# Cross-attention over 32 batches: value rows loaded in padded runs of 80 per head

## The chip, the cores and the metric

The kernel runs on one core of a Trainium2 chip. The time is the device time of one execution in microseconds (us), given as the median of several runs. A profiled execution, taken by the hardware profiler, shows what each engine did: PE multiplies matrices (PEld loads its weights), DVE, ACT and POOL work on vectors, SP issues the DMA transfers. The transfers of the core share 16 DMA engines.

## The reference

The input x is (32, 512, 640), the context (32, 77, 1024), in float32. With 20 heads of 32 columns:

```python
q = _heads(hidden_states @ to_q_w)
h_txt = _sdpa(q, _heads(ehs_txt @ to_k_w), _heads(ehs_txt @ to_v_w))
...
out = _merge(h_txt) + SCALE_OBJ * _merge(h_obj) + SCALE_OTH * _merge(h_oth) + SCALE_IP * _merge(h_ip)
out = out @ to_out_w + to_out_b
out = (out + residual) / RESCALE
```

where `_sdpa` is softmax(q k^T / sqrt(32)) v. The context has 77 rows per batch, all of which are the text part, so the object, other and image parts are empty and add zero. What remains is one attention over 77 keys per batch, a projection with bias, and the residual x.

## The kernel before, in words

Every float32 operand of a product is split into a high and a low part (`split`: ACT copies the high part, DVE or POOL subtracts it), and a product is three passes: high by high, high by low, low by high (`PAIRS`).

First stage, about the first 280 us: keys and values of all 32 x 77 = 2464 context rows, in groups of 512 rows. Weights and context are loaded (`split_weights` L103, `context` L132), the context is transposed on DVE, PE computes keys (L164) and values (L190), and both go back to memory as `k_dram` and `v_dram`. `v_dram` holds, for each row, 20 heads x 32 columns x (high, low); one head of one row is 256 bytes in one piece. This stage is ordered by a scheduler in the framework. It begins with a tile of zeros, set by DVE (L211), with which PE does twelve products that nobody reads (`warm`, L214).

Second stage: the instructions are in an order written out by hand (`manual_schedule`, L639). A slot is one batch b and one chunk j of four heads; n = 5 b + j counts 160 slots. Each engine works through its own list in this order, and SP issues all DMA transfers in this order too; an instruction that waits holds all behind it on its engine. A slot n contains, among others:

- `refill` (L507): loads of keys (`kb`) or values (`vb`) of the batch. The five chunks are in two groups (`GROUPS`: chunks 0 and 1, chunks 2 to 4), each with one buffer. At j = 1 the values of group 0 are loaded, at j = 3 those of group 1, at j = 0 and j = 2 keys.
- `cast_p` (L395) and `rest_p` (L402): the probabilities of slot n - 3, read back into `raw`, are split into `pp` by ACT (L399, L405), DVE (L406) and POOL (L409).
- four times `scores` (L329): PE computes 128 queries x 308 scores into one of three buffers `sc`, DVE takes the negated maximum per head (`nm`, L343). Behind each, `exps` (L348): ACT computes the exponentials into `pn` (L353), and their sums. The buffer `sc` comes free after that.
- `sums` and `normalize` (L361, L366): POOL divides the probabilities of slot n - 1 by their sums (L368), behind POOL's part of `rest_p`.
- `queries` (L311) of slot n + 1 on PE, `split_q` to ACT and DVE.
- `finish` (L475): DVE adds the projected rows to the residual (L481), SP stores finished rows (`out_dram`, L485). `load_residual` (L439) loads x rows into one of three buffers `xr`, POOL adds the bias (L446).
- `load_p` (L388): the probabilities of slot n - 2 are loaded from memory into `raw` (L391, L392).
- `transpose_p` (L372): DVE transposes the probabilities of slot n - 1 in blocks (`z`, L375), and four stores (L382) write them to a buffer `pd` in memory, from where `load_p` gets them with keys as rows. Each head has 80 rows there (KPAD), 77 for the keys and three of zeros: `pn` is cleared once and only 77 of its 80 columns are written.
- `values` (L417): PE multiplies `pp` with `vb` (eight passes, L423).
- `piece` (L467): PE's share of the output projection of an earlier batch (L453).
- `transpose_x` (L259) at j = 0 and 1: DVE transposes parts of x of the next batch in place, in the buffer `xs` (L261); `split_x` (L263) at j = 1 to 3 splits it. `load_x` (L251) at j = 4 loads x of the batch after the next into `xs` with four transfers (L256), behind the stores and loads of that slot.

The tile `vb` has 128 rows and, per chunk, three blocks: the 4 x 80 padded rows of the four heads fill blocks 0 and 1 and half of block 2; the other half of block 2 repeats those rows, for the low part of the probabilities. It is cleared once. `load_values` loads it by `SEGMENTS`, seven pieces of rows that belong to one head and one block:

Of the kernel before, what the change touches and what calls it, by code (L numbers as in the profile page):

```python
# [8 lines left out]
F32 = mybir.dt.float32  # L9
FPR = mybir.dt.float32r  # L10
# [13 lines left out]
P = 128  # L24
Q = 32
HEADS = 20
HD = 32
NKEY = 77
HPC = 4
KCOLS = HPC * NKEY  # L30
KPAD = 80
# [5 lines left out]
for _t in range(3):  # L37
    for _i in range(HPC):
        _lo = max(_t * P, _i * KPAD)
        _hi = min((_t + 1) * P, _i * KPAD + NKEY)  # L40
        if _lo < _hi:
            SEGMENTS.append((_t, _lo - _t * P, _i, _lo - _i * KPAD, _hi - _lo))
            if _t == 2:
                SEGMENTS.append((_t, _lo - _t * P + 64, _i, _lo - _i * KPAD, _hi - _lo))
# [6 lines left out]
def kernel(  # L51
# [24 lines left out]
    nc = tc.nc  # L76
    B, S, C = x.shape
    CA = ehs.shape[2]
    NT = B * NKEY
# [11 lines left out]
    dram = ctx.enter_context(tc.tile_pool(name="scratch", bufs=1, space=DRAM))  # L91

    k_dram = dram.tile([P, NC_, 2, NT], FPR, name="k_dram")
    v_dram = dram.tile([NT, HEADS, HD, 2], FPR, name="v_dram")
    wo_dram = dram.tile([P, NC_, 2, C], FPR, name="wo_dram")

    bias = const.tile([P, C], F32, name="bias")
# [111 lines left out]

    zero = kvt.tile([P, G], FPR, name="zero", tag="craw")  # L210
    nc.vector.memset(zero.bitcast(F32), 0.0)  # L211
    warm = psk.tile([P, G], F32, tag="ps", name="warm")
    for _ in range(12):
        nc.tensor.matmul(warm, zero[:, :P], zero, start=True, stop=True)  # L214
# [500 lines left out]
```

## Time and profile before

| | |
|---|---|
| time, median of 3 runs | 2177.66 us (2176.08 to 2178.84) |
| profiled execution | 2178.59 us |
| its span, first to last instruction | 2176.8 us |
| PE busy | 2043.0 us (94%) |
| ACT busy | 1377.9 us (63%) |
| DVE busy | 1230.4 us (57%) |
| POOL busy | 1051.7 us (48%) |
| 16 DMA engines, the queue of the loads and stores | 72.9% |
| mean granted clock of PE | 0.971 of full speed |

Busy time is that in which an engine works on an instruction. Idle time of an engine that isn't the bottleneck costs nothing; it has to be followed to the engine that loses by it. Where the profile names a releaser (`<- DMA raw<-pd`), it is the one that ended the idle time before the instruction. An engine `SPq` in the answers is SP's queue of issues: the duration there is that of the issue, not of the transfer. "x7" is a count of like instructions in a row.

### The profile page before, as it was taken

What the parts mean: (1) busy time and instruction counts of PE and PEld (TensorE: products, weight loads), DVE (VectorE), ACT (ScalarE), POOL (GpSimd) and SP (SyncE); (2) the same over time, 40 slices, a digit from 0 to 9 for tenths busy, and PEclk for the clock granted to TensorE, in tenths of its full rate; (3) what the DMA queues carried; (4) which work ended last, traced back from release to release, by engine and by line L of the source; (5) the groups of instructions that cost most, each with busy time, mean ns of one, the idle gap of its engine ahead of it and who ended that gap; (6) DMA issues with size and microseconds to landing.
All of it is one profiled execution on the core that took longest, in us unless ns stands there. A gap on an engine that the chain in (4) does not pass through costs nothing.

```text
span 2176.8 us, 37127 instructions
## 1 busy us (share of the span) xinstructions
PE 2043.0 (94%) x11012; PEld 1830.7 (84%) x11012; DVE 1230.4 (57%) x1996; ACT 1377.9 (63%) x6057; POOL 1051.7 (48%) x618
## 2 busy tenths in 40 slices
PE   8899997999999999999999999999999999999998
PEld 7799976888889888888888888888888888888897
DVE  5433245565556666656666655656556665656663
ACT  3322156666767776666777766767667766767772
POOL 0000034555556555555555555555555555555553
PEclk9999998999999999999999999999999999999999
DMA  8953359777777777777778777777777777777765
GB/s 189 266 173 110 106 120 237 193 195 191 191 205 192 197 199 194 199 193 195 189 208 209 205 193 191 202 187 201 208 188 197 198 194 198 194 199 186 208 183 171
DMA packets 524249, 416.51 MB, mean 191 GB/s; under 512 B 138480, under 2 KB 427760, under 8 KB 524048
## 3 DMA queue, kind: packets, MB, share of 16 engines
q1 hardware_dynamic: 524048, 414.13, 72.9%
q8 instruction: 90, 1.47, 0.3%
q14 instruction: 111, 0.91, 0.1%
HBM read 238.69 MB, written 175.31 MB: 190 GB/s over the span
## 4 chain that ended last, share of the span: by engine, by line
PE 37%; DMA 23%; SPq 13%; POOL 10%; ACT 6%; issue 6%; DVE 4%; POOLq 0%; DVEq 0%; ACTq 0%
DMA raw<-pd 11%; PE po L453 10%; DMA xs<-in_x_dram 9%; PE pq L317 8%; PE pk L164 5%; PE pa L423 5%; PE sc L335 5%; POOL pn L368 5%; PE pv L190 5%; POOL pp L409 4%; SPq L304 3%; ACT pn L353 3%; SPq L442 3%; SPq L256 3%; SPq L382 2%
## 5 line engine op out<-in xcount | busy, mean ns | idle before, releaser
L353 ACT ACTIVATE pn<-sc,nm 128x77 f32<-128x77 f32 x2560 | 801.3, 333 | 315.7 <-DVE nm L343 310.5
L453 PE MATMUL po<-wo_s,at 128*128 128x320 f32 x3840 | 645.3, 319 | 4.4 <-DVE xr L481 2.9
L409 POOL TENSOR_TENSOR pp<-raw,pp 64x512 fp32r<-64x512 f32 x160 | 280.8, 1755 | 701.5 <-ACT pp L405 701.5
L317 PE MATMUL pq<-xt,wq_s 128*128 128x512 f32 x2400 | 611.7, 395 | 2.3 <-ACT xt L268 1.3
L453 PEld LDWEIGHTS po<-wo_s,at 128*128 128x128 f32 x3840 | 604.3, 197 | 6.5 <-DVE xr L481 4.3
L353 ACT ACTIVATION_READ_ACCUMULATOR pn<-sc,nm 128x1 f32 x2560 | 539.8, 211 | 0.0
L317 PEld LDWEIGHTS pq<-xt,wq_s 128*128 128x128 f32 x2400 | 436.5, 188 | 83.7 <-POOL xt L269 3.0
L335 PE MATMUL sc<-kb,qt 128*128 128x308 f32 x1920 | 385.5, 310 | 85.4 <-ACT pn L353 84.4
L335 PEld LDWEIGHTS sc<-kb,qt 128*128 128x128 f32 x1920 | 326.4, 191 | 138.1 <-ACT pn L353 98.0
L368 POOL TENSOR_TENSOR pn<-pn,rs 128x1232 f32<-128x1232 f32 x160 | 364.2, 2276 | 30.3 <-DVE rs L363 18.1
L423 PE MATMUL pa<-pp,vb 128*128 128x512 f32 x1280 | 345.3, 410 | 24.0 <-ACT pp L399 14.1
L343 DVE TENSOR_REDUCE nm<-sc 128x4 f32<-128x308 f32 x640 | 287.8, 455 | 45.8 <-PE sc L335 45.2
L423 PEld LDWEIGHTS pa<-pp,vb 128*128 128x128 f32 x1280 | 250.0, 203 | 74.9 <-DVE pp L406 18.9
L406 DVE TENSOR_TENSOR pp<-raw,pp 128x1024 fp32r<-128x1024 f32 x160 | 196.0, 1225 | 203.9 <-ACT pp L399 203.9
L375 DVE STREAM_TRANSPOSE z<-pn 128x1280 f32<-128x1280 f32 x160 | 241.9, 1512 | 91.4 <-POOL pn L368 90.0
L269 POOL TENSOR_TENSOR xt<-xs,xt 128x512 fp32r<-128x512 f32 x160 | 204.6, 1292 | 113.3 <-ACT xt L268 105.9
L399 ACT CAST pp<-raw 128x1024 fp32r<-128x1024 f32 x160 | 168.3, 1052 | 139.7 <-DMA raw<-pd 137.5
L446 POOL TENSOR_TENSOR xr<-xr,bias 128x640 f32<-128x640 f32 x128 | 201.7, 1576 | 1.2 <-DMA xr<-in_x_dram 1.1
L101 DVE TENSOR_TENSOR qt<-pq,qt 128x512 fp32r<-128x512 f32 x160 | 110.6, 691 | 148.9 <-ACT qt L100 148.5
L261 DVE STREAM_TRANSPOSE xs<-xs 128x640 f32<-128x640 f32 x128 | 105.5, 826 | 147.1 <-DMA xs<-in_x_dram 140.7
L164 PE MATMUL pk<-ct,wk_s 128*128 128x512 f32 (+1 forms) x600 | 135.6, 386 | 12.3 <-ACT ct L100 12.3
L100 ACT CAST at<-pa 128x512 fp32r<-128x512 f32 x160 | 98.3, 614 | 70.0 <-PE pa L423 69.2
(36 smaller groups left out, 1164.1 us busy)
## 6 DMA issues: line engine op xcount, KB each, us to landing
pd<-z SPq DMA_DIRECT2D x640, 160.0 KB
raw<-pd SPq DMA_DIRECT2D x160, 512.0 KB
xs<-in_x_dram SPq DMA_DIRECT2D x128, 320.0 KB
xr<-in_x_dram SPq DMA_DIRECT2D x128, 320.0 KB
out_dram<-xr SPq DMA_DIRECT2D x128, 320.0 KB
raw<-pd SPq DMA_DIRECT2D x160, 128.0 KB
v_dram<-vs SPq DMA_DIRECT2D x19, 640.0 KB
k_dram<-ks SPq DMA_DIRECT2D x20, 512.0 KB
```

Source lines behind the costliest of these rows:

```text
L164: nc.tensor.matmul(pks[j][:, :gn], wk_s[:, k, a, j * P : (j + 1) * P], cts[k][:, c, :gn], start=(k == 0 and n == 0), stop=(k == NK - 1 and ...
L269: nc.gpsimd.tensor_tensor(parts[1], src, parts[0].bitcast(F32), ALU.subtract)
L317: nc.tensor.matmul(pqs[n], wq_s[:, k, a, j * P : (j + 1) * P], xts[b, k][:, c, :], start=(k == 0 and m == 0), stop=(k == NC_ - 1 and m == 2),)
L335: nc.tensor.matmul(sc[:, :KCOLS], qt[:, a, t * P : (t + 1) * P], kb[:, c, :], start=(m == 0), stop=(m == 2),)
L343: nc.vector.tensor_reduce(nm, sc[:, :KCOLS].rearrange("p (h k) -> p h k", k=NKEY), AX.X, ALU.max, negate=True)
L353: nc.scalar.activation(pnb[n % 2][:, at, :NKEY], sc[:, i * NKEY : (i + 1) * NKEY], AF.Exp, bias=nm[:, i : i + 1], accum_out=sms[n][:, at : ...
L368: nc.gpsimd.tensor_tensor(pf, pf, rs.unsqueeze(2).to_broadcast([P, NQ * HPC, NKEY]), ALU.mult)
L375: nc.vector.transpose(z.rearrange("p b t j -> p t b j"), pn.rearrange("p (t h) k -> p t (h k)", t=NQ).rearrange("p t (b i) -> p t b i", i=Q),)
L409: nc.gpsimd.tensor_tensor(pp[64:, 4, :], raw[:64, 2, :], pp[:64, 4, :].bitcast(F32), ALU.subtract)
L423: nc.tensor.matmul(pas[n], vb[:, t, :, a], pp[:, c, :], start=(m == 0), stop=(m == len(PASSES) - 1),)
L446: nc.gpsimd.tensor_tensor(xrs[b, t], xrs[b, t], bias, ALU.add)
L453: nc.tensor.matmul(pos[b, t, h][:, :HALF], ats[b * NC_ + j][:, a, t * P : (t + 1) * P], wos[0][:, j, c, h * HALF : (h + 1) * HALF], start= ...
```

## The change

The pieces that `load_values` loads get the three padded rows behind each head's 77. Their limits are now (i + 1) x 80 in place of i x 80 + 77: the seven pieces have 80, 48, 32, 80, 16, 64 and 64 rows in place of 77, 48, 29, 77, 16, 61 and 61. The rows 77 to 79 of a head are those of the first three keys of the next batch; the probabilities that they meet are zero. Behind the last batch `v_dram` gets three more rows, and a store of 15 KB from the tile `zero` fills them with zeros. In the built program this store is SP's third transfer, after two of the weight loads; but for it and the row counts, every engine has the same instructions in the same order.

```diff
         _lo = max(_t * P, _i * KPAD)
-        _hi = min((_t + 1) * P, _i * KPAD + NKEY)
+        _hi = min((_t + 1) * P, (_i + 1) * KPAD)
         if _lo < _hi:
...
-    v_dram = dram.tile([NT, HEADS, HD, 2], FPR, name="v_dram")
+
+    v_dram = dram.tile([NT + KPAD - NKEY, HEADS, HD, 2], FPR, name="v_dram")
...
     zero = kvt.tile([P, G], FPR, name="zero", tag="craw")
     nc.vector.memset(zero.bitcast(F32), 0.0)
+    nc.sync.dma_start(
+        v_dram[NT:].rearrange("n h d a -> (n h d a)").rearrange("(p u) -> p u", u=P).bitcast(F32),
+        zero[: (KPAD - NKEY) * HEADS * HD * 2 // P, :P].bitcast(F32),
+    )
     warm = psk.tile([P, G], F32, tag="ps", name="warm")
```

## The prediction

> **What bounds the kernel now.** I read the page's busy shares first: PE 94% of the span, DMA queue 72.9%, nothing else above 63%. So time can only be won where PE stands still or runs slowly. The table of waits says where PE stands still, and what else waits for transfers (columns: total us, times, longest):
>
> ```profile
> ACT pn L353 <- DVE nm L343: 310.5, 124, 9.1
> ...
> DVE xs L261 <- DMA xs<-in_x_dram: 140.7, 30, 5.9
> ACT pp L399 <- DMA raw<-pd: 137.5, 69, 5.1
> ...
> PE sc L335 <- ACT pn L353: 84.4, 31, 4.8
> ```
>
> 84.4 us in 31 gaps: that is one gap per batch. Listing the gaps between matmuls in the trace gives 29 of them from 415.2 to 2039.0 us, all in the first slot (j = 0) of a batch, together 82.9 us (2.86 each). The batch period between the gaps is (2039.0 - 415.2)/28 = 58.0 us. The timelines of the engines around one gap show what it hangs on (start, duration, instruction, idle before it):
>
> ```profile
> 1055.69 0.84 DVE L261 STREAM_TRANSPOSE xs<-xs 128x640 f32<-128x640 f32 x1 [4.64 <-DMA xs<-in_x_dram]
> ...
> 1056.84 0.46 DVE L343 TENSOR_REDUCE nm<-sc 128x4 f32<-128x308 f32 x1
> ```
> ```profile
> 1057.33 0.33 ACT L353 ACTIVATE pn<-sc,nm 128x77 f32<-128x77 f32 x1 [7.37 <-DVE nm L343]
> ```
> ```profile
> 1058.72 0.99 PE L335 MATMUL sc<-kb,qt 128*128 128x308 f32 x3 [3.00 <-ACT pn L353]
> 1059.51 3.20 PE L453 MATMUL po<-wo_s,at 128*128 128x320 f32 x12
> ```
>
> DVE stands in order behind a transpose of xs, which waits for the x load; the row maxima come late, so the exponentials, so the three score buffers, so PE. The following po group takes 3.20 us for 12 matmuls, 1.92 elsewhere. The clock column of the windows (PE, PEld, DVE, ACT, POOL busy; clock; DMA share; GB/s) says why:
>
> ```profile
> 1055.70:1058.70 3.00, 0.02 (x1) 0.00 (x0) 2.94 (x5) 1.34 (x8) 0.00 (x0) 1.00 1.05 292
> 1058.90:1062.30 3.40, 3.40 (x14) 3.40 (x15) 2.06 (x5) 2.75 (x11) 1.05 (x1) 0.50 0.47 108
> ```
>
> Half clock for 3.4 us, straight behind the gap. The clock record has 23 such dips behind the 29 gaps (19 of 3.4 us, 4 of 6.8 us).
>
> Why is the x load late? It was issued at 1044.85, in the order of SP's queue. I went back one slot in SP's, ACT's and POOL's timelines:
>
> ```profile
> 1019.25 2.26 SPq L382 DMA_DIRECT2D pd<-z  x4
> 1021.61 5.33 SPq L304 DMA_DIRECT2D vb<-v_dram  x7
> 1026.99 2.51 SPq L442 DMA_DIRECT2D xr<-in_x_dram  x1
> 1029.60 0.39 SPq L391 DMA_DIRECT2D raw<-pd  x1
> ...
> 1044.85 2.65 SPq L256 DMA_DIRECT2D xs<-in_x_dram  x4
> ```
> ```profile
> 1034.34 1.05 ACT L399 CAST pp<-raw 128x1024 fp32r<-128x1024 f32 x1 [3.60 <-DMA raw<-pd]
> ...
> 1036.03 1.75 POOL L409 TENSOR_TENSOR pp<-raw,pp 64x512 fp32r<-64x512 f32 x1 [5.36 <-ACT pp L405]
> ...
> 1037.86 2.27 POOL L368 TENSOR_TENSOR pn<-pn,rs 128x1232 f32<-128x1232 f32 x1
> ```
> ```profile
> 1025.00:1030.00 5.00, 5.00 (x31) 4.68 (x31) 3.96 (x6) 3.85 (x16) 5.00 (x4) 1.00 0.10 22
> ```
>
> The loads of vb for group 1 (slot j = 3) leave the queue at 10% for 5 us. The load of raw behind them is late, the cast in slot 4 waits 3.60 us for it, POOL's subtraction and its normalization behind that are as late, then the transpose z (1040.17), the four stores pd (1041.71), the output store (1044.06) and the x load. In the whole trace the cast in slot j = 4 is preceded by 3.55 us of idle ACT on average (31 batches), in the other slots by 0.17 to 0.36. PE itself does not wait in slots 1 to 4 beyond 0.33 us per batch: it works on while the chain of the other engines falls behind, and pays in slot 0. So the cycle vb, raw, pp, pn, z, pd, xs sets the period of 58.0 us, with PE some 4 us faster.
>
> **Part 1: the rows of the loads.** Seven loads per group before, seven after, with 369 and 384 rows (times two or three heads of 256 bytes). At 4% more bytes nothing would be gained. The trace's list of packets shows more: from 1025.3 to 1030.0 only 256-byte packets start, 71 per us, one every 14 ns, each 18 ns long: one engine works. The Trainium skill ("DMA: Bandwidth & Descriptors", section on why a DMA increments its semaphore by 16) says that the number of engines is the largest up to 16 that divides the slowest dimension on both sides: 77 rows run on 11, 29 and 61 rows on 1, 48 and 16 on 16. The trace bears it out: the table of issues has 2,241 DMAs; were all on 16 engines, they would leave 35,856 semaphore packets of 4 bytes. By the rule 128 loads of 77 rows lose 5 each, 64 of 29 rows and 128 of 61 rows lose 15 each, 3,520 together, so 32,336; the trace has 32,337. The first engine gets for group 1 three times (7 + 7 + 3 + 29 + 1 + 61 + 61) = 507 packets, 7.1 us at 71 per us, for group 0 338, 4.8 us. After, 80, 48, 32, 80, 16, 64, 64 all divide by 16: 24 rows per engine, 72 packets (1.0 us) and 48 (0.7 us).
>
> A rule of the same page speaks against the change: its rules for kernel authors say that under 64 KB one pays mostly a fixed cost per transfer. All seven loads are under 64 KB (at most 57.8 KB), their number stays, so by that rule the sum is zero and the time 2177. The row of 5 us at 10% share decides: the cost of these loads is not fixed, it follows the packets on one engine.
>
> What that is worth in slots 3 and 4. Undisturbed issues take SP 0.42 to 0.50 us. SP starts the seven at 1021.61, is through at 1024.8 (before 1026.95: the last took 2.2 us), with xr at 1025.3 (before 1029.5), so raw is issued 4.3 us earlier. On the queue: pd runs to 1023.2, vb to about 1026 (seven issues, not 1.0 us of data, set that), xr 1.2 us, raw 2 us: 1029.2; before, the cast started 1.3 us after the last packets of raw: 1030.5. ACT was free at 1034.34 - 3.60 = 1030.74. So the wait is gone, and the chain moves by the whole 3.6 us: z to 1036.5, pd to 1038, output to 1040.4, x load to 1041.3. DVE has its transpose at 1052.1, the exponentials run at 1053.7, score buffers come free at 1055.1, while PE comes to need them at 1055.72. The gap closes with 0.6 us to spare. As the gaps scatter (0.4 to 4.8 us, mostly 2.4 to 3.4) and PE reaches the place sooner when it isn't slowed, I leave 0.4 us per batch.
>
> The sum:
> - gaps in slot 0: -82.9 us.
> - left over, 0.4 x 29: +11.6 us. Bounds: 0, and 1.0 x 29 = 29 us.
> - half clock behind them. The Trainium skill ("TensorE: Matmul & The Clock Gate", the terms table) prices it as throttled time x (1 - K/N): (19 x 3.4 + 4 x 6.8) x 0.5 = 46 us. The rows say less: from the end of a gap to the next one PE took 54.8 us with a 3.4 us dip (1000.8 to 1055.7, 1058.7 to 1113.5), 55.8 with one of 6.8 (1869.0 to 1924.8), and 54.0 without (1519.5 to 1573.5, 1173.1 to 1227.1): 0.8 and 1.8 us. I take the rows: 19 x 0.8 + 4 x 1.8 = 22 us. The gaps of 0.4, 0.8 and 1.1 us had no dip behind them, and PE ran from 100 to 200 us gapless at a clock of 1.00, so neither the small gaps nor denser work should bring dips: -22 us.
> - the waits of pa in slot 4 for pp: 5.3 us over 28 batches: -5.5 us.
> - group 0's loads (slot 1; the share is 0.07 from 1061.4 to 1064.4): the cast in slot 2 waits 0.36 us, hidden from PE: 0. They add slack if the cover is gone.
> Together -98.8 us. The new period is then about 54.6 us.
>
> **Part 2: zeros.** One store of 15 KB stands third in SP's queue, between two weight loads each side. It waits for the memset (0.485 us long, behind a wait of 0.9, done at 1.4), and SP gets there at 1.6: no wait. The chain at the start is SP's issues, 0.42 us each; all loads behind it, k weights and context, move by one issue: +0.5 us. Below nothing is excluded (the store does no work that was done before); the upper end is a transfer's latency in the chain, some 3 us. The next user of its buffer is a transpose after 11 us.
>
> **Part 3: order.** No other instruction changes its place on any engine; the products with rows 77 to 79 meet zeros of pn. Nothing waits for later values: they are stored before slot 4, long before batch 1 loads.
>
> **Sum against the execution.** The profiled execution took 2178.59 us (span 2176.8 and 1.8 around it), 0.9 above the median 2177.66. 2178.6 - 98.8 + 0.5 = 2080.3; against the median 2079. I say 2080.
>
> **Rivals.**
> (a) Another transfer takes the place of the stall. The 1.3 MB x load itself takes 1047 to 1055 with the queue at 1.15 of its share, and raw in slot 4 waited for the landing of an output store (1034.28 to 1037.39). If the chain moves by 1.8 us instead of 3.6, gaps of about 1.3 us remain and half of the dips: 82.9 x 0.55 + 11 = 57 off, less small terms: 2125. For it: from 1045 to 1059 the queue is full. Against: it is empty from 1037 to 1038, and it empties in the slot before.
> (b) The stall is hidden: some other wait holds slot 4 and raw comes no earlier, or loads still run on few engines. Then 2178. Against it: idle ACT of 3.55 us in slot 4 alone.
> (c) Slower: the store of zeros. If the loads behind it in SP's queue were held until it has landed, the first k products would come later, and with nothing won in the loop the end would move by that. It decides from 4.4 us on; a store's latency (3 us, twice, as k weights and context are both held) gives 6 us, 2184. Against it: SP gets to it after the memset.
>
> **How the numbers follow.** Likeliest 0.76, with its own range from 2178.6 - 83 - 34 - 5.5 = 2056 (no gap left, dips midway between row and rule) to 2106 (1.0 us left and a third of the dips). (a) 0.18, 2106 to 2150; (b) 0.03; (c) 0.03. Faster 0.94, within 0.2% (4.4 us, about what a measurement of this kernel can tell from no change) 0.03, slower 0.03. The range, 2054 to 2128, takes the likeliest case nearly whole and half of (a).
>
> **What would show it.** Right: 35,871 packets of 4 bytes (all loads on 16 engines, the store's 30 rows on 15); no stretch at 0.1 share behind L304; L304's seven issues in about 3.2 us and L442 in 0.43; idle ACT before the slot 4 cast near zero; the wait of sc for pn under 25 us; clock above 0.985; period 54 to 55 us. Wrong: the wait of ACT for raw stays (step on SP's issue or on landing wrong), or it goes and PE still waits 2 us in slot 0 (the x load's step wrong), or the gaps go and dips come all the same.

## The result, and the profile after

The changed kernel takes 2077.69 us (median of 4 runs, 2073.90 to 2077.84), the kernel before on the same chip 2178.25 us. The ratio is 0.953, with a 95% interval from 0.951 to 0.955: 4.7% faster. The prediction was 2080, its range 2054 to 2128. The profiled execution took 2073.90 us, the fastest of the four; its span is 2072.1 us against 2176.8.

| | before | after |
|---|---|---|
| PE busy, share of the span | 94% | 97% |
| mean granted clock of PE | 0.971 | 0.988 |
| period of a batch | 57.96 us | 54.77 us |
| idle PE before the scores, slot j = 0, per batch | 2.86 us | 1.02 us |
| idle ACT before the cast in slot j = 4, mean | 3.55 us | 0.69 us |
| time at half clock in the loop | 92 us | 17 us |
| packets of 4 bytes | 32,337 | 35,872 |

The period is the mean over 29 batches, from the first exponential of slot 10 to that of slot 155. These 29 batches are called the loop in what follows. A stall is the stretch in which loads of vb on one engine hold up what stands behind them on the queue.

In the table of waits (total us, times, longest), the line numbers are five higher than before:

```profile
DVE xs L266 <- DMA xs<-in_x_dram: 129.7, 30, 6.0
...
ACT pp L404 <- DMA raw<-pd: 40.3, 48, 3.0
...
PE sc L340 <- ACT pn L358: 29.9, 20, 4.1
```

ACT waits 40 us for raw in place of 137.5, PE 30 us for score buffers in place of 84. DVE waits for the x load as long as before (129.7 and 140.7): that wait did not get shorter, it got earlier with all that surrounds it.

SP's queue around slot j = 3 of a batch, then ACT in slot 4 (start, duration, instruction, idle before it):

```profile
972.86 2.22 SPq L387 DMA_DIRECT2D pd<-z  x4
975.18 5.22 SPq L309 DMA_DIRECT2D vb<-v_dram  x7
980.44 0.60 SPq L447 DMA_DIRECT2D xr<-in_x_dram  x1
981.14 0.39 SPq L396 DMA_DIRECT2D raw<-pd  x1
...
996.54 2.70 SPq L261 DMA_DIRECT2D xs<-in_x_dram  x4
```
```profile
986.02 1.06 ACT L404 CAST pp<-raw 128x1024 fp32r<-128x1024 f32 x1 [1.67 <-DMA raw<-pd]
```

From the first of the seven loads to the load of raw it is now 6.0 us (before 8.0), to the x load 21.4 us (before 23.2). The seven issues themselves still take 5.2 us here, 4.4 on average (before 5.4): SP did not get as quick as I had taken it to be. The issue of xr behind them did get quicker: 0.60 us, where it was held for 2.51. This batch is one of the five that still have a dip of the clock. Three windows of it follow, then the gap that is left and PE behind it:

```profile
979.00:981.00 2.00, 2.00 (x11) 1.68 (x11) 1.38 (x2) 1.84 (x11) 2.00 (x2) 1.00 0.13 26
1008.70:1011.30 2.60, 0.03 (x1) 0.03 (x1) 2.54 (x6) 1.42 (x9) 0.00 (x0) 0.99 1.07 272
1011.30:1014.70 3.40, 3.40 (x13) 3.40 (x14) 3.05 (x6) 3.40 (x16) 1.83 (x2) 0.50 0.31 72
```
```profile
1008.24 0.84 DVE L266 STREAM_TRANSPOSE xs<-xs 128x640 f32<-128x640 f32 x1 [5.49 <-DMA xs<-in_x_dram]
```
```profile
1011.27 1.14 PE L340 MATMUL sc<-kb,qt 128*128 128x308 f32 x3 [2.71 <-ACT pn L358]
1012.21 3.03 PE L458 MATMUL po<-wo_s,at 128*128 128x320 f32 x12
1015.08 1.10 PE L428 MATMUL pa<-pp,vb 128*128 128x512 f32 x4
```

The stretch at a tenth of the queue is 2 us and not 5, and it is not packets on one engine any more. The seventh issue took 1.48 us in this batch, its median over the loop is 0.61. In the trace's list of packets a 16 KB packet of the queue that the profile calls `instruction` starts 0.03 us into it and takes 1.05 us. In four of the 29 batches one of the last five issues was held like this, for 1.5 to 1.9 us, each time with such a packet at its beginning. In these four, ACT waits 1.71 us on average before the cast in slot 4, in the other 25 0.58 us, and their gaps make 11.4 of the 29.5 us that are left. That the two come together is shown, not that the packet is the cause.

The gap in slot 0 is of the same kind as before, rarer and shorter: 18 gaps over 0.25 us in the loop where there were 29, 29.5 us where there were 82.9. Five dips of the clock are left of 23.

The span by stages, from the first exponentials of slots 0, 10, 155 and 159:

| stage | before | after | difference |
|---|---|---|---|
| to slot 0 | 291.6 | 289.1 | -2.5 |
| slots 0 to 9 | 113.0 | 106.3 | -6.7 |
| 29 batches | 1680.8 | 1588.2 | -92.6 |
| slots 155 to 158 | 44.1 | 40.9 | -3.2 |
| to the end | 47.3 | 47.6 | +0.3 |

The first row isn't the change: the changed kernel in another run came to slot 0 at 292.6 us.

### The profile page after: what moved, and what is told of

The parts are those of the page before. It is cut to its first block, busy times and chain, and to the rows that moved or that the text cites. A ratio compares the mean times of both kernels' runs of the same rounds, so it can differ in the third digit from the quotient of the medians.

```text
span 2072.1 us, 37128 instructions
## 1 busy us (share of the span) xinstructions
PE 2006.0 (97%) x11012; PEld 1804.7 (87%) x11012; DVE 1233.7 (60%) x1996; ACT 1383.4 (67%) x6057; POOL 1052.5 (51%) x618
## 4 chain that ended last, share of the span: by engine, by line
PE 61%; DMA 13%; SPq 7%; POOL 6%; ACT 4%; DVE 4%; issue 3%; POOLq 0%; DVEq 0%; ACTq 0%
PE po L458 17%; PE pq L322 16%; PE pa L428 9%; PE sc L340 8%; DMA xs<-in_x_dram 7%; PE pk L165 6%; PE pv L191 5%; DMA raw<-pd 5%; POOL pn L373 3%; POOL pp L414 3%; ACT pn L358 2%; SPq L261 2%; SPq L387 2%; DVE z L380 1%; SPq L309 1%
## 5 line engine op out<-in xcount | busy, mean ns | idle before, releaser
L458 PE MATMUL po<-wo_s,at 128*128 128x320 f32 x3840 | 623.3, 312 | 4.4 <-DVE xr L486 3.0
L458 PEld LDWEIGHTS po<-wo_s,at 128*128 128x128 f32 x3840 | 581.4, 190 | 7.6 <-DVE xr L486 5.1
L340 PE MATMUL sc<-kb,qt 128*128 128x308 f32 x1920 | 380.0, 307 | 30.9 <-ACT pn L358 29.9
L428 PE MATMUL pa<-pp,vb 128*128 128x512 f32 x1280 | 334.9, 403 | 14.7 <-ACT pp L404 11.6
L266 DVE STREAM_TRANSPOSE xs<-xs 128x640 f32<-128x640 f32 x128 | 105.5, 826 | 136.2 <-DMA xs<-in_x_dram 129.7
```

What stands on the lines that cost most here:

```text
L340: nc.tensor.matmul(sc[:, :KCOLS], qt[:, a, t * P : (t + 1) * P], kb[:, c, :], start=(m == 0), stop=(m == 2),)
L428: nc.tensor.matmul(pas[n], vb[:, t, :, a], pp[:, c, :], start=(m == 0), stop=(m == len(PASSES) - 1),)
L458: nc.tensor.matmul(pos[b, t, h][:, :HALF], ats[b * NC_ + j][:, a, t * P : (t + 1) * P], wos[0][:, j, c, h * HALF : (h + 1) * HALF], start= ...
```

## The experiments

A ratio is to the kernel before on the same chip, with its 95% interval. On the chips of the experiments the kernel before took some 2186 to 2191 us, so ratios are compared, not times; where an expectation gives a time, it is on the scale of 2178 us. All these kernels compute the whole result.

### Which of the two groups

```diff
-        for t, r0, i, k0, kn in SEGMENTS:
+        for t, r0, i, k0, kn in SEGMENTS if g == 1 else SHORT_SEGMENTS:
```

`SHORT_SEGMENTS` has the pieces of 77 rows. First with group 1 alone padded:

> Only the loads of group 1 (slot j = 3) have the padded rows, those of group 0 have 77 again; the store of zeros stays. Theory: only the stall in slot 3 is on the cycle that sets the period, the one in slot 1 is hidden. So nearly the whole gain: 2078, at most 2088; idle ACT before the cast in slot 4 under 1 us, and a stretch of about 3 us at a DMA share near 0.07 in slot 1. Rival (a fixed cost or the row count of each load matters, wherever it stands): gains go by the number of loads or their bytes, so half to three fifths of it, 2118 to 2128.

Measured: 0.9546 (0.9520 to 0.9571), a period of 55.19 us, idle ACT before the cast in slot 4 of 0.62 us.

With `g == 0`, group 0 alone:

> Only the loads of group 0 (slot j = 1) have the padded rows. Theory: 2170 (2162 to 2178), the stall of slot 3 stays and with it 3.5 us of idle ACT before the cast in slot 4 and 2.9 us of idle PE per batch. Rival (every load counts alike): 2128 to 2138.

Measured: 0.9912 (0.9889 to 0.9934), period 57.65, idle ACT in slot 4 still 3.50 us, idle PE in slot 0 still 2.79 us per batch. The loads of slot 3 carry nearly all of the gain, those of slot 1 under 1%. Group 0 alone, some 2159 on the scale of 2178, gained a little more than I had expected (2162 to 2178). The idea that every load counts alike (0.972 to 0.977 each) is out.

### Other numbers of rows

The limit of a piece is 78, then 79 rows per head:

```diff
-        _hi = min((_t + 1) * P, (_i + 1) * KPAD)
+        _hi = min((_t + 1) * P, _i * KPAD + 79)
```

> 78 rows per head in place of 80: pieces of 78, 48, 30, 78, 16, 62, 62 rows. Theory (the engine with the most packets sets the time): by the rule of the largest divisor up to 16 they run on 13, 16, 15, 13, 16, 2 and 2 engines; the first engine has 3 x (6 + 3 + 2 + 6 + 1 + 31 + 31) = 240 packets for group 1, 3.4 us at 71 per us, which hides behind the 5 us that SP takes to issue seven loads, except for the 2.6 us of the last two. 2080 to 2095. Rival (only loads on all 16 engines help): near 2178. Rival (the row count itself): the gain of a third, 2145.

> 79 rows per head: pieces of 79, 48, 31, 79, 16, 63, 63 rows, more bytes than 77 and fewer than 80. Theory: 79 and 31 rows run on one engine, 63 on 9, so the first engine has 3 x (79 + 3 + 31 + 79 + 1 + 7 + 7) = 621 packets for group 1 against 507 with 77 rows: 8.7 us against 7.1, 1.6 us more in each of 29 periods, 46 us: 2224 (2200 to 2245), slower than with 77 rows. Rival (row count, padding or alignment of the runs): between 77 and 80 rows, 2080 to 2110.

Measured: 78 rows 0.9552 (0.9529 to 0.9574), 79 rows 1.0587 (1.0556 to 1.0617). Padding with two rows in place of none makes the kernel 5.9% slower, with one or three 4.5 to 5% faster. Neither the bytes nor the rows nor the number of loads can do that; the number of engines by the divisor does. The packets of 4 bytes confirm that number in each case: 33,632 with 78 rows and 32,096 with 79, where the divisors give 33,631 and 32,095 (in both as in the kernels before and after, the trace has one more). Times from the first of the seven issues on, for group 1, mean issue times and medians of the rest:

| | 77 rows | 78 | 79 | 80 |
|---|---|---|---|---|
| packets on the first engine, worked out | 507 | 240 | 621 | 72 |
| seven issues | 5.37 us | 3.85 | 9.68 | 4.41 |
| to the last packet | 9.54 us | 6.99 | 11.12 | 5.52 |
| to the issue of raw | 8.08 us | 5.49 | 10.17 | 5.05 |
| period | 57.96 us | 55.11 | 62.30 | 54.77 |

The last packet comes 1.58 us later with 79 rows than with 77; the working was 114 packets at 71 per us, 1.6 us. That part fits. What it costs does not: I had put 1.6 us on the period, it is 4.3. SP's queue with 79 rows:

```profile
1068.36 9.77 SPq L309 DMA_DIRECT2D vb<-v_dram  x7
1078.17 0.36 SPq L447 DMA_DIRECT2D xr<-in_x_dram  x1
1078.63 0.39 SPq L396 DMA_DIRECT2D raw<-pd  x1
```

With a load on one engine ahead of them, issues are held here: the loads behind the first piece of 79 rows and behind that of 31 rows took 3.68 and 3.25 us to issue (means for group 1). The way from the loads of group 1 to the x load is 2.4 us longer (25.86 against 23.48), and the way from the loads of group 0 to those of group 1 is 1.9 us longer (23.98 against 22.09), where the stall of slot 1 now shows: the cast in slot 2 waits 2.26 us, before 0.32. And half clock in the loop rose from 92 to 133 us.

### The two parts of the change apart

The loads without the store: the last batch loads 77 rows (`LAST_SEGMENTS`), `v_dram` has no rows behind it.

```diff
-        for t, r0, i, k0, kn in SEGMENTS:
+        for t, r0, i, k0, kn in SEGMENTS if b + 1 < B else LAST_SEGMENTS:
...
-    nc.sync.dma_start(
-        v_dram[NT:].rearrange("n h d a -> (n h d a)").rearrange("(p u) -> p u", u=P).bitcast(F32),
...
```

> The padded loads alone: the last batch loads 77 rows as before, and there are no rows of zeros and no store of them. Theory: the same as the changed kernel less one issue at the start, 2077 (2073 to 2081). Rival (the store at the start or what it shifts has a share in the gain): 2085 or more.

The store without the loads is the changed kernel with `_i * KPAD + NKEY` as the limit again.

> The store of zeros alone, all loads with 77 rows. Theory: 0.5 us more at the start, 2178.7 (2174 to 2183), no difference that a measurement tells. Rival (it delays the weight loads by its landing): 2184 or more; rival (the 2.5 us that the changed kernel is ahead by the first slot come from it): 2175 or less, with slot 0 starting 2 us earlier.

Measured: loads alone 0.9474 (0.9450 to 0.9499) at 2076.65 us, store alone 0.9979 (0.9964 to 0.9993). The changed kernel once more, for the comparison:

> The changed kernel once more, on the chip of the two runs beside it, so that they can be compared: the ratio to the kernel before as measured first, 0.953 (0.951 to 0.955), and by the theory the same within 0.3% as the padded loads alone.

Measured: 0.9492 (0.9478 to 0.9507), 2077.48 us; the interval of the ratio lies a little below that of the first measurement, and on the scale of 2178 both this run (2067) and the loads alone (2064) are below what was expected: the kernel before is some 10 us slower on these chips, the changed kernel is not. The loads are the gain; the store is not slower than nothing. That it should be faster by 0.07 to 0.36%, as its interval says, has no step that I could find. It comes to 2174 on that scale, which the second rival allows (2175 or less), but slot 0 does not start 2 us earlier as that rival needs: it starts at 291.4 us against 291.6, and the idle PE in the loop is 85.5 us against 82.9. The loads alone agree with the whole change within 0.1% in their medians (2076.65 and 2077.48, on two chips), which speaks against a share of the store.

### Engines without padding

No row more than 77 per head; each piece is cut into a multiple of 16 and the rest, twelve loads in place of seven.

```diff
+            _mid = _lo + (_hi - _lo) // 16 * 16
+            for _a, _b in ((_lo, _mid), (_mid, _hi)):
...
```

> 77 rows as before, not a row more, but each piece is cut into a multiple of 16 rows and the rest of 13: 64 + 13, 48, 16 + 13, 64 + 13, 16, 48 + 13 twice, twelve loads in place of seven. Theory (packets on the first engine): 16 and 13 engines, at most 3 x 24 = 72 packets on one, so the stall is gone; SP issues five loads more, 2.3 us per group, which eats much of it. 2100 (2085 to 2125). Rival (a fixed cost per load of a small transfer): slower than before, 2190 or more. Rival (it is the padding that helps): 2178 or more.

Measured: 0.9906 (0.9872 to 0.9939), some 2157 on the scale of 2178, where I had expected 2100. The sign rules out both rivals, and the packets of 4 bytes are as the divisors give them (40,017 for 40,016). The size was wrong because of SP:

```profile
1009.70 6.31 SPq L308 DMA_DIRECT2D vb<-v_dram  x12
1016.05 0.36 SPq L446 DMA_DIRECT2D xr<-in_x_dram  x1
1016.50 0.39 SPq L395 DMA_DIRECT2D raw<-pd  x1
```

The last packet comes 7.31 us after the first issue, not far from the 6.99 of 78 rows. But twelve issues take 6.5 us and raw is issued after 6.82 us, against 5.49 with 78 rows; the same happens in slot 1. The period is 57.31 us against 55.11, in an execution that was the fastest of six (2155.80 us, the median is 2168.93). So raw issued 1.3 us later in slot 3, and 2.0 us later in slot 1 (7.8 us after the first issue against 5.8), goes with 2.2 us or more per period, though by the divisors no engine has more than 72 packets. Whether packets or issues hold SP back, what stands behind is late.

### The x load earlier

In the changed kernel, the x load of slot 4 stands behind the load of raw in place of behind the output store:

```diff
             load_p(n - LAG + 1)
+        if j == 4 and b + 2 < B:
+            load_x(b + 2)
...
-        if j == 4 and b + 2 < B:
-            load_x(b + 2)
```

> The changed kernel, with the four transfers of the x load (slot j = 4) moved ahead: behind the load of raw of that slot, before the four stores of pd and the output store. Theory: what is left of idle PE in slot 0 (29.5 us of gaps before the scores, five stretches at half clock) comes from the x load that starts late; it is now issued some 6 us earlier. Gaps nearly gone: 2045 (2038 to 2058). Rival: pd, the output store and the load of raw for slot 0 stand behind 6.5 us of x load, and the wait moves there: 2070 to 2095.

Measured: 0.9393 (0.9363 to 0.9422), 2057.56 us; loads alone, on the same chip in the same session, took 2076.65. This version is faster than both kernels. Its waits in the loop and its clock:

```profile
PE po L458 <- DVE xr L486: 11.9, 19, 1.5
...
PE sc L340 <- ACT pn L358: 2.8, 5, 0.8
```
```profile
core 0: 2053.6 us, clock 0.994
```

Idle PE before the scores is gone (0.1 us per batch), no dip of the clock is left in the loop, and the period is 54.08 us. The gap that the change had left was the x load coming late.

The same move in the kernel before, with 77 rows:

> The kernel before, with 77 rows, and the x load of slot j = 4 moved ahead of the stores of pd and the output store. Theory (the stall costs time only because the x load comes late through it, and PE pays in slot 0): the x load is issued some 5 us earlier, so idle PE before the scores goes from 2.9 us per batch to under 0.5 although ACT still waits 3.5 us before the cast in slot 4: 2090 (2075 to 2115) on the scale of 2178. Rival (the wait of ACT for raw in slot 4 is itself what costs): 2150 or more.

Measured: 0.9885 (0.9869 to 0.9902). My expectation fell, the rival's held. The waits in the loop:

```profile
ACT pp L399 <- DMA raw<-pd: 184.3, 82, 5.8
...
PE pa L423 <- DVE pp L406: 34.9, 55, 0.8
...
PE sc L335 <- ACT pn L353: 18.6, 19, 1.8
PE pa L423 <- ACT pp L399: 15.7, 20, 1.7
```

The gaps before the scores did close (18.6 us for 80.3 in the same window) and the clock went to 0.989, but the period only fell from 57.96 to 57.50 us. PE now waits before pa, for the split of raw (50.6 us, before 6.8). Idle PE is 2.98 us per batch, before 3.17, in smaller pieces over all slots. So the late x load is the place where PE met the delay, not the only way by which the delay reaches it.

### Raw ahead of the loads

The kernel before, with the loads of group 1 behind the loads of the residual and of raw of slot 3:

```diff
-        elif j == 3 and b >= 1:
-            load_values(b, 1)
...
             load_p(n - LAG + 1)
+        if j == 3 and b >= 1:
+            load_values(b, 1)
```

> The kernel before, with 77 rows, and the loads of group 1 in slot j = 3 moved behind the loads of the residual and of raw in that slot, ahead of the stores of pd. Theory: raw no longer stands behind the one engine, idle ACT before the cast in slot 4 falls from 3.5 us to under 0.7, but the stores of pd and the output store of slot 3 and the loads of slot 4 now stand behind it; half of the gain or more, 2110 (2085 to 2150). Rival (whatever stands behind the loads on the queue delays the chain as much): 2170 or more.

Measured: 0.9933 (0.9913 to 0.9953). Idle ACT before the cast in slot 4 is 0, as expected, but 2.59 us now stand before the cast in slot 0, where it was 0.02 (the prediction's 0.17 to 0.36 us for the slots other than 4 holds for slots 1 to 3 alone); the period is 57.70 us. The rival is nearly right: what stands behind the loads is late, whichever transfer it is, and the chain finds it one slot on. Moving the stall in the order gains 0.7%, taking it away 4.5%.

### What is left of group 0's stall

> Padded rows for group 1 alone (slot j = 3), the x load of slot j = 4 moved ahead. With 77 rows the early x load left a period of 57.5 us, with 2.9 us of PE idle spread over the slots and idle ACT of 3.9 us before the cast in slot 4 and 2.0 us before that in slot 2. Theory 1 (slot 3's stall is the one that costs, wherever the x load stands): as with all loads padded and x early, 0.939 to 0.945 of the kernel before, although the wait in slot 2 stays at 2 us. Theory 2 (once x is early, the stall of group 0 in slot 1 isn't hidden any more and costs as well): 0.95 to 0.97, with PE idle before pa in slot 2.

It is the first experiment's kernel with the x load moved as above. Measured: 0.9519 (0.9496 to 0.9543), at the lower end of the second expectation (0.95 to 0.97) and above the first. Idle ACT in slot 4 is 0.52 us, in slot 2 2.12 us, idle PE before pa in slot 2 0.65 us per batch, period 54.94. With the x load early, the three periods are 57.50 (both stalls), 54.94 (group 0's alone), 54.08 (none): the stall of slot 3 is worth 2.6 us and that of slot 1 0.9. With the x load late, group 0's was worth 0.4 (55.19 against 54.77). That the gap in slot 0 hid it fits these periods and the waits before pa; no run shows it more directly.

## Why the prediction was right, point by point

**One engine holds the queue: right.** 35,872 packets of 4 bytes, 35,871 worked out. The rule of the divisor told 78 from 79 rows as it told 77 from 80.

**Only the stall of slot 3 is on the path: right**, with a remainder. Group 1 alone gives 4.5%; group 0 alone 0.9%, where I had put nothing.

**The x load is 3.6 us earlier: too much.** The steps in the trace, as means over 28 batches:

| from to | before | after | predicted change | measured |
|---|---|---|---|---|
| first load of group 1 to the x load | 23.48 us | 20.73 us | -3.6 | -2.75 |
| x load to DVE's first transpose | 11.01 | 10.94 | 0 | -0.07 |
| to the loads of group 0 | 1.37 | 1.33 | 0 | -0.04 |
| to the next loads of group 1 | 22.09 | 21.77 | PE sooner | -0.32 |

The term that was mis-sized is SP's seven issues: I had 0.42 to 0.50 us each, 3.2 us in all. They take 4.41 us. Part of the reason is in the mean issue times for group 1: the pieces of 29 and 61 rows, on one engine, had been quick to issue (0.24 and 0.22 us); with 32 and 64 rows they take 0.39 and 0.61. Only the last of the seven, which was held for 2.24 us, got shorter (0.71). What stands behind the seven gained more: the issue of xr went from 2.54 us to 0.69. So raw is issued 3.0 us earlier in the median, not 4.3 (2.8 in the mean: 0.96 from the seven, 1.85 from xr), and ACT still waits 0.69 us.

**What is left of the gaps: 0.4 us per batch expected, 1.02 measured**, at the outer bound (1.0) that I had given. Gaps gave 53 us in place of 71.

**The half clock: the rule was nearer than my row.** One dip by itself shows it. PE in the kernel before, at full clock and then in the dip behind the gap that the prediction shows:

```profile
1049.04 0.59 PE L335 MATMUL sc<-kb,qt 128*128 128x308 f32 x3
1049.47 1.92 PE L453 MATMUL po<-wo_s,at 128*128 128x320 f32 x12
1051.22 0.59 PE L335 MATMUL sc<-kb,qt 128*128 128x308 f32 x3
...
1058.72 0.99 PE L335 MATMUL sc<-kb,qt 128*128 128x308 f32 x3 [3.00 <-ACT pn L353]
1059.51 3.20 PE L453 MATMUL po<-wo_s,at 128*128 128x320 f32 x12
1062.55 1.81 PE L423 MATMUL pa<-pp,vb 128*128 128x512 f32 x7
```

The three sc matmuls and the twelve po behind them, from the first start to the start of what follows, take 2.18 us at full clock (2.19 in the median of 266 such pairs in the loop) and 3.83 us in the dip. The dip of 3.4 us costs 1.6 us; the one in the changed kernel, at 1011.27 above, costs as much. My row had 0.8 us. The Trainium skill ("TensorE: Matmul & The Clock Gate", section "Terms") prices a dip at its throttled time x (1 - K/N), where K/N is the granted share of the clock, here one half: 1.7 us.

The whole loop says less clearly the same. PE's time per batch without its idle time fell from 54.79 us (57.96 less 3.17) to 53.61 (54.77 less 1.16): 1.18 us, 34 us in 29 batches. Half clock went from 92 to 17 us, 38 us by the rule and 18 by my stretches with and without dips. With the x load early, 92 us of dips went, 46 by the rule; PE's time fell by 1.39 us per batch (to 54.08 less 0.68), 40 us in all. But the kernel before with the early x load has 17 us of half clock too, and its PE time is 54.52 us (57.50 less 2.98), only 8 us less in 29 batches. There the weight loads wait some 45 us longer than the matmuls (from 420 to 2060 us; 20 us in the kernel before), and the difference above counts this as PE's work. So the size of the term rests on the single dips.

The stretches of 54.0 us without a dip were no clean measure of a loop without dips: in the changed kernel such stretches take 53.2 to 53.9 us (572.6 to 625.8, 1284.7 to 1338.6).

**The sum: close, and in part by luck.** The gaps gave 18 us less than I had put and the dips some 12 us more (by the difference in PE's time), which nearly cancel. In the loop, which holds all terms of the sum but the store's 0.5 us, the span fell by 92.6 us and not by 98.8. The rest of the 104.7 us came before and behind it, 6.7 us of it in slots 0 to 9, where the sum had nothing, and 2.5 us ahead of slot 0, which is scatter.

**The signs that I had named.** The packets, the clock (0.988) and the period came out as named. The wait of sc for pn is 29.9 us where I had named under 25, the seven issues take 4.41 us for 3.2, and the issue of xr 0.69 us for 0.43: all on the side of a smaller effect of the loads.

**A cost that goes by the number of transfers: no.** It would have made 2177 us. With the same seven transfers per group, 77, 78, 79 and 80 rows took 1, 0.955, 1.059 and 0.953 of the time.

**The zeros: not seen**, as expected. The store is issued at 1.65 us, for 0.46 us, and slot 0 starts where it did, within the scatter of 289 to 293 us.

**The rivals.** That another transfer takes the place of the stall (a) was right in kind: 1.02 us per batch are left by the x load, and moving it wins another 0.9%. The picture of one chain from vb over raw to the x load was too narrow. With the x load early and the stall in place, the time hardly fell; the delay came over raw and the split into pa. What is shown is that the queue's order carries the stall on to whatever stands behind it. Which path sets the period of 57.5 us there was not taken apart further.

## What to carry to other kernels

Count the engines of each transfer before its bytes: 61 rows ran on one of 16 engines, 64 on all (by the divisors, which the counted packets bear out), and the three added rows, which only meet zeros, took 4.7% off the whole kernel; 79 rows cost 5.9%. When a wait is seen far from a slow transfer, follow the order of the issuing queue back to it, and expect that moving it only moves the wait. Cutting a transfer into pieces that spread well is paid in issues, and padding was the cheaper way here.

## What the runs showed of the hardware that was not expected

- The loads of 29, 31 and 61 rows, on one engine, were quick to issue (0.22 to 0.24 us for group 1), those of 32 and 64 rows on 16 engines slow (0.39 and 0.61 us). The price of the first comes later, when issues behind them are held: 2.2 us behind 61 rows, 3.7 us behind 79.
- In four of 29 batches of the changed kernel an issue took 1.5 to 1.9 us in place of 0.5 or 0.6, each time together with a 16 KB packet of the `instruction` queue. The same kernel in another run has four such batches as well (1.0 to 1.7 us).
- The granted clock fell to half for 3.4 us behind gaps of 1.8 to 4.2 us in the changed kernel (five dips), but not behind others of 2.0 to 2.5 us. Without such gaps it did not fall at all in 29 batches, with PE at work for over 98% of the time: dense work was not what brought the dips. In the two kernels with 77 rows in some group and the x load early, the clock also fell behind two waits of 0.7 to 0.75 us that lay 1.2 to 1.3 us apart: a single long gap was not needed there.
- 1.6 us more on one engine cost 4.3 us per period (79 rows). The way over the x load got longer by 2.4 us and that from group 0's loads to group 1's by 1.9, and the time at half clock rose from 92 to 133 us.
